# A six-layer decoder on one core: another planner for the order of work, and the context's keys and values made ahead and kept in DRAM

## The chip, the cores and the metric

One Trainium2 chip, of which one core runs the program. TensorE (PE in the profile) does matrix products, VectorE (DVE), ScalarE (ACT) and GpSimd (POOL) do the rest, and SyncE (SP) issues the DMAs. The metric is device microseconds from start to end of one execution, the median of several runs.

## The reference

`x` holds 128 sequences of 64 tokens of 128 numbers, `ctx` the same for a context. Each of six layers adds to `x` something made of `layernorm(x)`:

```python
x = x + mamba2_block(ln(x))                 # scan over 64 steps, then an MLP with silu
x = x + pointers(ln(x), ctx, ids, ptr)      # three rows of ctx by pointer: scores, softmax, values
x = x + ternary_ffn(ln(x))                  # weights of -1, 0, 1; 8-bit activations; gelu
x = x + causal_attention_twice(ln(x))       # 16 heads; the second pass has its queries from a convolution of the first
x = x + cross_attention(ln(x), ctx, mask)   # 16 heads: q of x, k and v of ctx
x = x + experts(ln(x))                      # 8 experts, the two best weighted
```

In the pointers layer `k = ctx @ Wk.T` and `v = ctx @ Wv.T` for two sets of weights; the kernel folds them with the query and output weights into `wqk` and `wvo`. In cross attention `k = ctx @ wk`, `v = ctx @ wv`. These four products need the context alone, and nothing of `x`.

## The kernel before, in words

The 128 sequences are worked in 16 groups of 8 (512 tokens, four tiles of 128x128 in f32). A group goes through ten stages: prepare, project, recur and mlp (the Mamba layer), pointers, ternary, first, second (the two passes of causal attention), cross, experts. `way(g)` (L1603) loads x, calls the stages in turn and stores the result. Up to seven groups are under way at a time (seven buffers `x`), and a stage holds one group at a time: its name is a token that the next group must get.

Nothing at run time decides the order. While the program is built, a class `Turns` (L85) plays the groups against each other, each as a Python generator. `yield V, 0.8` asks for an engine for a planned time in us; `yield "a"` takes a token (a buffer, one of four PSUM banks `a`, the stage's name), `turns.give("a")` hands it back; `yield None, 2.5` lets planned time pass, for a DMA; `yield [p, q]` starts parts side by side. Whoever is chosen issues its instructions at that moment, so that each engine's queue, and SP's queue of DMAs, is written in the order of this play. Each engine then works its queue strictly in that order, held back by semaphores where data or buffers are not ready. The planned lengths are written in by hand (`dv`, `ac`, `po` and literals such as 0.88 for one 128x512 product). Among those who want an engine the planner takes first those who hold a scarce token (`a`, or `s`, the four banks of scores), then the one whose request was made earliest (`process["n"]`); a token goes to whoever asked first.

What the change touches:

- pointers, `group(g)` (L781): takes `ctxT` and one of the two buffers `u`, loads the group's context into it (L786), turns it into `ctxT` by four transposes (`turning`, L317 and L319), stores that in a DRAM tensor `contexts` (L802), makes `kT` by two 128x512 products (`keys`, copied out by ACT at L812) and `vo` by 32 small ones (`outputs`, L828). Beside this the same stage builds one-hot rows on DVE and does the layer norm of x (L307 and L308 on DVE, L286 and L287 and L325 on POOL, then transposes).
- cross, `group(g)` (L1417): loads the mask (L1421), takes `ctxT` and loads it from `contexts` (L1427), makes `km` by one product and two ACT passes (`spreading`, L1086) and `v` by four products (`values`, L214 and L216); beside it the norm and the queries.
- All matrix products are issued in one helper, so that they have the line L210; they are told apart by their tiles.
- project: `arows` is stored to a DRAM tensor `steps` (L484), read back spread over all partitions into four tiles `pT` (L506), which DVE then scans (L530); L572 multiplies the result by a product of PE's.

The buffers `u` are two, shared by the context's load and by all layer norms; from recur to mlp one is held throughout.

Of the kernel before, what the change touches and what calls it, by code (L numbers as in the profile page):

```python
# [32 lines left out]
P = 128  # L33
# [51 lines left out]
class Turns:  # L85
# [5 lines left out]

    LAG = 0.2

    def __init__(self, tokens, scarce=()):
        self.scarce = scarce
        self.free = {name: [0.0] * n for name, n in tokens.items()}
        self.wanted = {name: [] for name in tokens}
        self.asked, self.until, self.now, self.n = {}, {}, 0.0, 0

    def give(self, name):  # L100

        self.running["scarce"] = max(0, self.running["scarce"] - (name in self.scarce))
        if self.wanted[name]:
            _, process = self.wanted[name].pop(0)
            process["time"] = max(process["time"], self.now)
            process["scarce"] += name in self.scarce
            process["engine"] = None
            self.ready.append(process)
        else:
            self.free[name].append(self.now)  # L110

    def process(self, work, time, parent):
        return dict(work=work, time=time, parent=parent, scarce=0, engine=None, n=0)

    def step(self, process):
        self.running = process
        while True:
            self.now = process["time"]
            item = next(process["work"], None)
            self.n += 1  # L120
# [9 lines left out]
            if isinstance(item, str):  # L130
                if not self.free[item]:
                    self.wanted[item].append((self.n, process))
# [11 lines left out]
            else:  # L144
# [9 lines left out]
                else:  # L154
                    process["engine"], process["n"] = engine, self.n
                self.asked.setdefault(engine, []).append((process["scarce"] < 1, process["n"], process, length))
                return

    def run(self, works):
        self.ready = [self.process(work, 0.0, None) for work in works]  # L160
        while True:
# [3 lines left out]
            for engine, asked in self.asked.items():  # L165
                if asked:
                    at = max(self.until.get(engine, 0.0), min(r[2]["at"] for r in asked))
                    first = min((r for r in asked if r[2]["at"] <= at), key=lambda r: r[:2])
# [6 lines left out]
            process, length = request[2:]  # L175
            self.until[engine] = at + length
            process["time"] = at + length + self.LAG
            self.step(process)
        assert not any(self.wanted.values()), {k: v for k, v in self.wanted.items() if v}


@with_exitstack
def tile_decoder(ctx: ExitStack, tc: tile.TileContext, w: dict, const: bass.AP, out: bass.AP):
    nc = tc.nc
    V, A, G, T = nc.vector, nc.scalar, nc.gpsimd, nc.tensor
# [15 lines left out]
    TOKENS.update({name: int(i < 4) for i, name in enumerate(LAYERS)})  # L201
    counter = [0]
# [32 lines left out]
    nc.sync.dma_start(cst, const)  # L235
# [7 lines left out]
    contexts = dram.tile([NG * P, GT], F32, tag="contexts", name="contexts")  # L243
# [17 lines left out]
    for name, v in rows:  # L261
        r = v.shape[0] // P
        nc.sync.dma_start(vrow[at : at + r, :], v.rearrange("(r p) -> r p", p=P))
# [7 lines left out]
    def broadcast(pool, name, ap, n):  # L271

        t = pool.tile([P, n], F32, tag=f"bc_{name}", name=f"bc_{name}")
        nc.sync.dma_start(t, ap.partition_broadcast(P))
        return t

    def load(name, shape, ap, pool):
        t = pool.tile(shape, F32, tag=name, name=name)
        nc.sync.dma_start(t, ap)
# [80 lines left out]
    def natural(shape, ap):  # L360

        t = wk(shape, "pT", bufs=BUFS["pT"])
        nc.sync.dma_start(t, ap)
# [5 lines left out]
    def mamba(mp):  # L369
# [8 lines left out]
        nc.sync.dma_start(taps, w["L0_attn_conv_w"][0:256, :].rearrange("(b p) k -> p b k", p=P))  # L378
# [5 lines left out]
        for i in range(2):  # L384
            rows, of = slice(32 * i, 32 * i + 16), slice(256 + 16 * i, 272 + 16 * i)
            V.tensor_copy(wbc[:, rows], win[:, 512 + 16 * i : 528 + 16 * i])
            nc.sync.dma_start(tbc[rows, :], w["L0_attn_conv_w"][of, :])
            nc.sync.dma_start(bcb[rows, :], w["L0_attn_conv_b"][of].unsqueeze(1))
# [10 lines left out]
        for h in range(4):  # L399
            nc.sync.dma_start(  # L400
# [4 lines left out]
        steps = dram.tile([NC * 4, P], F32, tag="steps", name="steps")  # L405
# [7 lines left out]
        def prepare(g):  # L413
# [70 lines left out]
            nc.sync.dma_start(steps[g * C * 4 : (g + 1) * C * 4, :], rows)  # L484
# [14 lines left out]
        def project(g):  # L499
# [4 lines left out]
            for c in range(C):  # L504
                at = (g * C + c) * 4
                nc.sync.dma_start(  # L506
# [217 lines left out]
    def pointers(mp):  # L724
# [5 lines left out]
        nc.sync.dma_start(pi, w["itok_BxS_0_4092"].rearrange("(c b) s -> c (b s)", b=2))  # L730
        nats = {}
        for names in (("Wout", "Wkj", "Wqj", "Wvj"), ("Wki", "Wqi", "Wvi")):
            t = wk([P, 4, P], "pT", bufs=BUFS["pT"])
            for i, name in enumerate(names):
                nc.sync.dma_start(t[:, i, :], w[f"L0_xattn_{name}"])
# [45 lines left out]
        def group(g):  # L781

            yield "ctxT"
            yield "u"
            cg = wk([P, C, P], "u", bufs=BUFS["u"])
            nc.sync.dma_start(cg, tokens(cf, g))  # L786
            ctxT = wk([P, GT], "ctxT", bufs=BUFS["ctxT"])
            idg = wk([P, C, S], "idg", I32)
            for b in range(2):
                nc.sync.dma_start(  # L790
                    idg[b * S : (b + 1) * S], ids[b, g * C : (g + 1) * C, :].partition_broadcast(S)
                )
            kT = wk([P, B, 2, S], "kT")
            vo = wk([P, B, P], "vo")
            hot = wk([P, 3, C, S], "hot")
            rid = sm([P, C], "rid")

            def context():
                yield None, 2.5
                yield from turning(ctxT, [cg[:, c, :] for c in range(C)])  # L800
                turns.give("u")
                nc.sync.dma_start(contexts[g * P : (g + 1) * P, :], ctxT)  # L802
                yield [keys(0), keys(1), outputs(0), outputs(1)]
                turns.give("ctxT")

            def keys(i):
                yield "a"
                pk = bank("a")
                yield T, 0.88
                mm(pk, wqk[:, i, :], ctxT)  # L810
                yield A, ac(512)
                A.copy(kT[:, :, i, :], pk.rearrange("p (b s) -> p b s", s=S))  # L812
                turns.give("a")

            def outputs(half):
                yield "a"
                pvo = bank("a")
                yield T, 0.95
                for j in range(4):
                    b = half * 4 + j  # L820
                    for i in range(2):
                        mm(
                            pvo[i * S : (i + 1) * S, j * P : (j + 1) * P],
                            ctxT[:, b * S : (b + 1) * S],
                            wvo[:, i, :],
                        )
# [828 lines left out]
```

## Time and profile before

| | |
|---|---|
| median of 3 runs | 2220.43 us (2209.86 to 2229.43) |
| the profiled execution | 2218.08 us, of which the span from first to last instruction is 2216.3 |
| mean granted TensorE clock | 0.931 |
| PE busy | 1925.3 us, 87% of the span |
| PE loading weights (PEld; it overlaps PE) | 1363.1 us, 62% |
| DVE, ACT, POOL busy | 1489.0, 1158.7, 1020.8 us |
| moved by DMA | 53.61 MB, 24 GB/s over the span |

How to read it: engines work side by side, so that busy times do not add up. Idle time of PE is what separates the span from PE's work. A granted clock below 1 means that products of that stretch ran slower than they can. Shares over the whole span hide that the first quarter, in which groups enter one after the other, differs from the rest.

### The profile page before, as it was taken

Reading aid. Unit: us, or ns where it says so; the run is one execution under the profiler, and the core shown is the slowest. Engines: PE = TensorE matmul, PEld = TensorE weight load, DVE = VectorE, ACT = ScalarE, POOL = GpSimd, SP = SyncE. Lnnn points to the kernel's source line nnn. Section 1 sums busy time; section 2 is a strip of 40 time slices with the busy share of each in tenths; the row PEclk is TensorE's granted clock in tenths of the full one; section 3 lists DMA queues with packets and bytes.
Section 4 is the critical chain, followed back from the end, with each engine's and each line's share of the span. In section 5 each row is a group of like instructions: output and inputs, shape, how many; then the busy total and the mean of one; then the engine's idle time right before and its main releaser. Section 6 shows DMA issues by size and latency. Waiting matters only on the chain.

```text
span 2216.3 us, 56830 instructions
## 1 busy us (share of the span) xinstructions
PE 1925.3 (87%) x23920; PEld 1363.1 (62%) x23920; DVE 1489.0 (67%) x3991; ACT 1158.7 (52%) x2133; POOL 1020.8 (46%) x1258
## 2 busy tenths in 40 slices
PE   3777788889889989999998898989889999997996
PEld 1455556566656666666666576666556666675664
DVE  4577877675685676786776847777676765745353
ACT  2345456556464566556565464555655555553452
POOL 2566754743444444364545552464544533423121
PEclk9688898999999999999999899999899999998998
DMA  5011010000010010010001000000000000000000
GB/s 164 20 51 36 28 38 2 23 7 18 22 36 12 6 47 21 16 37 15 26 23 38 6 28 21 16 19 26 28 25 24 2 25 11 17 7 6 12 6 5
DMA packets 73451, 53.61 MB, mean 24 GB/s; under 512 B 30087, under 2 KB 59757, under 8 KB 73197
## 3 DMA queue, kind: packets, MB, share of 16 engines
q1 hardware_dynamic: 73196, 49.99, 7.6%
q8 instruction: 188, 3.08, 0.6%
q14 instruction: 67, 0.54, 0.1%
HBM read 41.45 MB, written 8.52 MB: 23 GB/s over the span
## 4 chain that ended last, share of the span: by engine, by line
PE 55%; DVE 26%; POOL 6%; ACT 6%; issue 3%; DMA 3%; SPq 1%; DVEq 0%; POOLq 0%; ACTq 0%
PE psa L210 38%; PE pss L210 12%; PE psa L317 4%; DVE tops L1212 4%; POOL u L325 2%; DVE amx L1167 2%; DVE pT L1155 2%; DVE x L1581 2%; DVE st L307 1%; ACT pT L1245 1%; DVE mv L308 1%; DVE sel L863 1%; DMA x<-in_x 1%; DVE s L870 1%; DVE mx L1030 1%
## 5 line engine op out<-in xcount | busy, mean ns | idle before, releaser
L325 POOL TENSOR_SCALAR u<-x,mv,rstd 128x128 f32<-128x128 f32 x320 | 252.8, 802 | 52.3 <-PE psa L317 26.0
L210 PE MATMUL psa<-fT,moe_w 128*128 128x512 f32 x512 | 257.8, 627 | 11.3 <-ACT km L559 3.1
L210 PEld LDWEIGHTS psa<-moe_w,hid 128*128 128x128 f32 x2048 | 242.5, 193 | 28.6 <-issue 19.1
L210 PE MATMUL psa<-moe_w,hid 128*128 128x128 f32 x2048 | 252.0, 279 | 2.4 <-DVE sel L863 1.7
L1559 ACT ACTIVATE hid<-psa,vcol 128x512 f32<-128x512 f32 x256 | 173.5, 689 | 147.2 <-PE psa L210 144.4
L1581 DVE SCALAR_TENSOR_TENSOR x<-psa,cw,x 128x128 f32<-128x128 f32 x512 | 143.3, 342 | 127.6 <-PE psa L210 127.5
L1169 POOL TENSOR_TENSOR pT<-pT,amx 128x512 f32<-128x512 f32 x128 | 134.6, 1055 | 185.9 <-DVE amx L1167 177.9
L286 POOL TENSOR_SCALAR rsq<-mv 128x4 f32<-128x4 f32 x96 | 24.7, 257 | 368.6 <-DVE mv L308 346.1
L1245 ACT ACTIVATE pT<-pss 128x512 f32<-128x512 f32 x256 | 132.1, 603 | 118.8 <-PE pss L210 118.7
L1212 DVE TENSOR_REDUCE tops<-pss 128x32 f32<-128x2048 f32 x64 | 146.1, 2283 | 41.3 <-PE pss L210 41.3
L1044 POOL TENSOR_SCALAR r<-h 128x512 bf16<-128x512 f32 x64 | 98.0, 1540 | 128.2 <-DVE h L1042 127.0
L210 PEld LDWEIGHTS psa<-fT,moe_w 128*128 128x128 f32 x512 | 91.3, 198 | 100.2 <-issue 59.4
L1289 DVE TENSOR_TENSOR fT<-psa,inv 128x256 f32<-128x256 f32 x96 | 40.2, 420 | 155.2 <-ACT inv L1287 154.2
L210 PEld LDWEIGHTS pss<-km,qm 32*128 32x128 f32 x3072 | 101.4, 198 | 46.7 <-issue 31.5
L210 PE MATMUL psa<-pT,cst 128*32 128x256 f32 x1536 | 119.6, 401 | 10.4 <-ACT pT L1245 2.9
L625 POOL TENSOR_TENSOR qm<-qm,km 128x256 f32<-128x256 f32 x64 | 51.6, 809 | 165.6 <-DVE qm L620 165.5
L317 PE MATMUL psa<-cst,u 128*128 128x128 f32 x448 | 83.9, 304 | 50.1 <-POOL u L325 33.9
L210 PE MATMUL pss<-km,qm 32*128 32x128 f32 x3072 | 120.6, 297 | 5.6 <-DVE pT L1155 3.5
L307 DVE BATCH_NORM_STATS2 st<-x 128x6 f32<-128x128 f32 x384 | 102.7, 267 | 20.6 <-DMA x<-in_x 20.1
L319 ACT COPY fT<-psa 128x512 f32<-128x512 f32 x112 | 65.7, 588 | 85.2 <-PE psa L317 84.8
L317 PEld LDWEIGHTS psa<-cst,u 128*128 128x128 f32 x448 | 56.0, 151 | 78.2 <-POOL u L325 43.3
L1285 ACT ACTIVATE inv<-psa 128x256 f32<-128x256 f32 x96 | 37.0, 385 | 125.9 <-PE psa L210 125.5
(282 smaller groups left out, 4621.3 us busy)
## 6 DMA issues: line engine op xcount, KB each, us to landing
pT<-steps SPq DMA_DIRECT2D x64, 256.0 KB, 4.0
x<-in_x SPq DMA_DIRECT2D x16, 256.0 KB, 2.8
mask<-in_mask_Bx1xSxS_ff SPq DMA_DIRECT2D x32, 128.0 KB, 3.0
u<-in_ctx SPq DMA_DIRECT2D x16, 256.0 KB, 2.7
contexts<-ctxT SPq DMA_DIRECT2D x16, 256.0 KB, 2.0
ctxT<-contexts SPq DMA_DIRECT2D x16, 256.0 KB
out<-x SPq DMA_DIRECT2D x16, 256.0 KB, 2.3
idg<-in_itok_BxS SPq DMA_DIRECT2D x32, 64.0 KB, 2.8
```

Of the source, the lines that this page charges most:

```text
L210: T.matmul(o, lhsT=lhsT, rhs=rhs, start=start, stop=stop)
L307: V.bn_stats(st[:, c, :], X[:, c, :])
L317: T.transpose(pt[:, c * P : (c + 1) * P], part, by)
L319: A.copy(o, pt)
L325: G.tensor_scalar(u[:, c, :], X[:, c, :], mean(c), scale[:, c : c + 1], ALU.subtract, ALU.mult)
L625: G.tensor_tensor(xc[:, :, cols], xc[:, :, cols], zs[:, :, cols], ALU.mult)
L1044: G.tensor_scalar(r2, h[:, c, :], -MAGIC, None, ALU.add)
L1169: G.tensor_tensor(s3, s3, mx.unsqueeze(2).to_broadcast([P, 8, S]), ALU.subtract)
L1212: V.tensor_reduce(mx[:, :, 0:8], banks.rearrange("p r (n s) -> p r n s", s=S), AX.X, ALU.max)
L1245: A.activation(pTs[r].rearrange("p b g q -> p (b g q)"), banks[:, r, :], AF.Exp)
L1559: A.activation(hid[:, b, :], ph, AF.Relu, bias=vec["moe_b1"][:, 2 * e + b : 2 * e + b + 1])
L1581: V.scalar_tensor_tensor(X[:, c, :], po_[:, c * P : (c + 1) * P], cw[:, c, e : e + 1], X[:, c, :], ALU.mult, ALU.add,)
```

## The change

1. **Context ahead.** The stage pointers makes no keys any more. A new process `ahead()` goes through the 16 contexts on its own: load into a buffer of the tag `ctxT`, transposes, then `kT` and `vo` (for pointers) and `km` and `v_x` (for cross), each stored in a DRAM tensor of its own per group (4 KB a partition for `kT`, `vo` and `km`, 6 KB for `v_x`). The stages pointers and cross load these back. `contexts` is gone, and the context no longer takes a buffer `u`. One buffer each of `kT`, `vo` and `v_x` serves both sides, by tokens; `km` shares its four. A token `pointed{g}` or `crossed{g}` lets the stage of group g begin only when its tensors were made. `ahead` has rank 1, all groups have rank 0: it gets an engine or a token only where no group wants it, except while it holds a bank.
2. **Planning with TensorE's clock.** The planner cuts time into stretches of 3.413 us; a product of PE's is planned at half speed unless PE was planned busy for 0.74 of the stretch before.
3. **Allowances.** Requests are ordered by rank, then by the time at which they are made plus an allowance of the layer. `planned` plays the whole program 150 times with allowances altered at random and keeps what ends earliest; in these plays the engines issue nothing (`Engine`, `Stand`). In the program built from it the allowances are: cross -19.2, recur -14.3, ternary -14.3, project -12.5, experts -5.6, mlp -5.2, first -0.8, second 0, pointers +6.2, prepare +6.7.

The number of products, and of all other instructions on PE, is the same in both. The diff, cut to its core (`nc.sync` is renamed to `Q` throughout):

```diff
     LAG = 0.2
+    STRETCH, ENOUGH = 3.413, 0.74
+    def taken(self, engine, at, length):
+        if engine is not self.clocked:
+            return length
+        t, left = at, length
+        while left > 1e-9:
+            i = int(t / self.STRETCH + 1e-9)
+            rate = 1.0 if self.worked.get(i - 1, 0.0) >= self.ENOUGH * self.STRETCH else 0.5
+            part = min((i + 1) * self.STRETCH - t, left / rate)
+            self.worked[i] = self.worked.get(i, 0.0) + part
+            left -= part * rate
+            t += part
+        return t - at
+    def layer(self, name):
+        self.running["allowance"] = self.allowances.get(name, 0.0)
...
-            _, process = self.wanted[name].pop(0)
+            first = min(self.wanted[name], key=lambda w: w[0])
...
+    def age(self, process):
+        self.n += 1
+        return process["rank"], process["time"] + process["allowance"], self.n
...
-            self.until[engine] = at + length
+            self.until[engine] = at + self.taken(engine, at, length)
...
+def planned(layers, names, rounds=150):
+    chance = random.Random(2)
+    best, end = {}, layers({})
+    for _ in range(rounds):
+        tried = dict(best)
+        for name in chance.sample(names, chance.choice((1, 2, 3))):
+            tried[name] = round(tried.get(name, 0.0) + chance.uniform(-15.0, 15.0), 1)
+        at = layers(tried)
+        if at <= end:
+            best, end = tried, at
+    return best
...
+    TOKENS.update(ctxT=1, kT=1, vo=1, v_x=1, laid=0)
+    TOKENS.update({f"{name}{g}": 0 for name in ("pointed", "crossed") for g in range(NG)})
...
@@ pointers: group(g) @@
-            yield "ctxT"
-            yield "u"
-            cg = wk([P, C, P], "u", bufs=BUFS["u"])
-            nc.sync.dma_start(cg, tokens(cf, g))
-            ctxT = wk([P, GT], "ctxT", bufs=BUFS["ctxT"])
+            yield f"pointed{g}"
+            yield "kT"
+            kT = wk([P, B, 2, S], "kT", bufs=1)
+            Q.dma_start(kT.rearrange("p b i s -> p (b i s)"), kept["kT", g])
+            yield "vo"
+            vo = wk([P, B, P], "vo", bufs=1)
+            Q.dma_start(vo.rearrange("p b d -> p (b d)"), kept["vo", g])
...
-            yield [context(), ones(), norming_T(xs[g], uT)]
+            yield [ones(), norming_T(xs[g], uT)]
...
@@ cross: of_context(g, ctxT), new @@
+        def of_context(g, ctxT):
+            def keys():
+                yield "km"
+                km = wk([P, B, 2, S], "km", bufs=BUFS["km"])
+                yield from spreading(km, wkk, ctxT, k["mk"], None)
+                Q.dma_start(kept["km", g], km.rearrange("p b i s -> p (b i s)"))
+                yield None, 3.0
+                turns.give("km")
+            def of_values():
+                yield "v_x"
+                yield from values(vs[0], ctxT, wv)
+                Q.dma_start(kept["v_x", g], vs[0])
+                yield None, 4.0
+                turns.give("v_x")
+            yield [keys(), of_values()]
+            turns.give(f"crossed{g}")
...
@@ cross: group(g) @@
-            yield "ctxT"
-            ctxT = wk([P, GT], "ctxT", bufs=BUFS["ctxT"])
-            nc.sync.dma_start(ctxT, contexts[g * P : (g + 1) * P, :])
+            yield f"crossed{g}"
+            yield "v_x"
             v = vs[0]
+            Q.dma_start(v, kept["v_x", g])
             yield "km"
             km = wk([P, B, 2, S], "km", bufs=BUFS["km"])
+            Q.dma_start(km.rearrange("p b i s -> p (b i s)"), kept["km", g])
...
+    def ahead():
+        def loaded(g):
+            cg = wk([P, C, P], "ctxT", bufs=2)
+            Q.dma_start(cg, tokens(cf, g))
+            return cg
+        yield "laid"
+        following = loaded(0)
+        yield None, 2.5
+        for g in range(NG):
+            cg = following
+            ctxT = wk([P, GT], "ctxT", bufs=2)
+            yield from turning(ctxT, [cg[:, c, :] for c in range(C)])
+            if g + 1 < NG:
+                following = loaded(g + 1)
+            yield [stages["pointers ahead"](g, ctxT), stages["cross ahead"](g, ctxT)]
...
-    turns.__init__(TOKENS, ("a", "s"))
+        turns.__init__(TOKENS, ("a", "s"), T, allowances)
...
-        turns.run([way(g) for g in range(NG)] + [weights()])
+        return turns.run([(0, way(g)) for g in range(NG)] + [(0, weights()), (1, ahead())])
```

## The prediction

> **What bounds the kernel now.** I read the page first, for busy shares and slices.
>
> ```profile
> span 2216.3 us, 56830 instructions
> PE 1925.3 (87%) x23920; PEld 1363.1 (62%) x23920; DVE 1489.0 (67%) x3991; ACT 1158.7 (52%) x2133; POOL 1020.8 (46%) x1258
> ...
> PE   3777788889889989999998898989889999997996
> DVE  4577877675685676786776847777676765745353
> ...
> PEclk9688898999999999999999899999899999998998
> ```
>
> PE is the bound, but not in the first eight slices, where it is busy seven or eight tenths at a lower clock. So the second view is a table of stretches: columns are us, busy time of PE, PEld, DVE, ACT, POOL, then the granted clock.
>
> ```profile
> 55.40:110.80 55.40, 39.01 (x147) 24.43 (x148) 30.40 (x92) 17.70 (x37) 31.48 (x39) 0.62 0.06 20
> 110.80:166.20 55.40, 40.99 (x243) 28.09 (x244) 44.03 (x114) 25.39 (x46) 33.59 (x45) 0.82 0.15 51
> 166.20:221.60 55.40, 41.98 (x245) 27.78 (x243) 43.67 (x109) 33.11 (x54) 38.61 (x50) 0.85 0.12 36
> ...
> 1551.40:1773.00 221.60, 198.33 (x2543) 141.98 (x2542) 157.56 (x422) 124.67 (x227) 109.43 (x135) 0.95 0.06 19
> 1773.00:1994.70 221.70, 207.69 (x3118) 150.01 (x3111) 134.40 (x341) 122.99 (x224) 77.41 (x86) 0.96 0.05 15
> ```
>
> The timeline of SP gives the cut between the two regimes: seven groups are let in at once, and the eighth gets its buffer x when the first is stored, at 560 us. Cut there, the table is:
>
> ```profile
> 0.00:560.00 560.00, 430.34 (x4524) 295.80 (x4525) 392.02 (x1046) 279.02 (x513) 303.39 (x383) 0.88 0.13 38
> 560.00:2216.30 1656.30, 1494.94 (x19398) 1067.30 (x19396) 1096.97 (x2946) 879.70 (x1621) 717.43 (x875) 0.95 0.07 19
> ```
>
> Before 560 us PE is idle for 129.7 us of 560 (23%), after it for 161.4 of 1656.3 (9.7%): the fill waits on the latency of single groups, the rest on PE. SP's timeline also shows a context at work: loaded into a buffer u (L786), stored when it has left it (L802).
>
> ```profile
> 560.20 0.39 SPq L1613 DMA_DIRECT2D out<-x  x1
> ...
> 580.40 0.37 SPq L786 DMA_DIRECT2D u<-in_ctx  x1
> 604.50 0.33 SPq L484 DMA_DIRECT2D steps<-arows  x1
> 606.96 1.76 SPq L506 DMA_DIRECT2D pT<-steps  x4
> ...
> 623.71 0.43 SPq L802 DMA_DIRECT2D contexts<-ctxT  x1
> ```
>
> Last, the groups by form that the context costs on PE (busy us, mean ns), and two DMAs (us to landing):
>
> ```profile
> L210 PE MATMUL psa<-wvo,ctxT 128*64 128x128 f32 x512 | 34.7, 288 | 2.3 <-DVE fT L1289 1.2 <-ACT kT L812 1.1
> L210 PE MATMUL psa<-ctxT,wqk 128*128 128x512 f32 x64 | 34.0, 646 | 2.4 <-ACT ctxT L319 2.0 <-ACT r2T L319 0.3
> L317 PE MATMUL psa<-cst,u 128*128 128x128 f32 x448 | 83.9, 304 | 50.1 <-POOL u L325 33.9 <-DVE u L678 10.0 <-DMA u<-in_ctx 2.6
> L210 PE MATMUL psa<-ctxT,x_wk 128*128 128x512 f32 x32 | 17.5, 627 | 0.0
> L210 PE MATMUL psa<-x_wv,ctxT 128*128 128x128 f32 x128 | 17.0, 275 | 0.0
> ```
>
> ```profile
> pT<-steps SPq DMA_DIRECT2D x64, 256.0 KB, 4.0
> ...
> contexts<-ctxT SPq DMA_DIRECT2D x16, 256.0 KB, 2.0
> ```
>
> **Part 1, context moved into the fill.** A group's context costs PE 34.0 + 34.7 + 17.5 + 17.0 us over 16 groups and 64 of the 448 transposes (83.9 / 7 = 12.0): 115.2 / 16 = 7.2 us, nothing of it new. What counts is where it stands. In PE's old order, ahead of group 7's first product (the 560 us mark), are the transposes, wqk and wvo of six contexts (80.7 / 16 x 6 = 30.3 us) and the cross part of two (34.5 / 16 x 2 = 4.3): 34.6. In the new order nine whole contexts are: 64.8. So 30.2 us of PE work leave the stretch in which PE is busy 90.3%: 30.2 / 0.903 = -33 us. In the fill they cost between 0 (all in PE's idle 129.7 us) and 30.2 / (430.34 / 560) = +39 (nothing hidden). I take +10: PE, ACT (32 to 60% busy in the three stretches) and POOL have room, DVE (79% in two of them) gets only the copies it had anyway.
>
> **Clock in the fill.** From 55 to 222 us PE is busy 122.0 us at a mean clock of 0.76; where it is busy over 83% it was granted 0.92 and more. With more work between, the clock can stay (0) or come to 0.95 (122 x 0.76 / 0.95: -24). I take -6, a quarter, since chains that wait on DVE win nothing. The Trainium skill (TensorE: Matmul & The Clock Gate, Part 1) has the clock at half unless a window of about 3.4 us was busy; by it, filling nearly every window would give the whole 24 and a sum 18 us lower. The trace agrees in that busier stretches have the higher clock (0.62 at 70% busy, 0.96 at 94%); that the gaps close, nothing here shows.
>
> **Part 2, order of the rest: clock in the plan, allowances, no u.** Allowances of -19 (cross) to +7 (prepare) make almost a ranking of the stages, as a request seldom waits that long. No row shows the new order, so I bound it by stretches. After 560 us 1494.9 - 30.2 = 1464.7 us of PE work are left: at 90.3% 1622 us, at the best stretch's share (207.69 / 221.7 = 93.7%) 1563, at the worst's (89.5%) 1637. So -59 to +15, middle -22. One thing speaks for the gaining side: from L786 to L802 a context held one of the two buffers u for 5 to 44 us (580 to 624 above), 262 us over 16, and PE's transposes wait 33.9 us for POOL to write u. I take -30.
>
> **DMA.** 128 transfers come (64 stores, 64 loads; 512 KB, for v_x 768) and 32 of 256 KB go. SP issues one in 0.4 us: 38 us more of SP's 2216, which is mostly waiting. By size from 4.0 us for 256 KB a load lands within 8, v_x within 12. They are covered: kT by the norm in the same stage (4 x (267 + 182) ns on DVE, 257 + 1049 and 4 x 802 on POOL, 4 x 304 transposes, 588 copy: 8.1 us); km by that and the queries; v by the scores and the softmax too. ACT's copies, DVE's and POOL's work are moved, not added. I take 0; without the cover each group's chain is some 4 us longer, 64 in all, part of the last rival.
>
> **Sum** against the profiled 2218.1 (2.3 below the median 2220.4): 2218.1 - 33 + 10 - 6 - 30 = 2159, say **2160**. The good ends together: 2218.1 - 33 + 0 - 24 - 59 = 2102; the bad ends: 2218.1 - 33 + 39 + 0 + 15 = 2239.
>
> **Rivals.**
> *Larger gain*: good ends, 2102. For it: idle and half clock are there to be had. Against it: the plan's lengths are still guesses (0.88 for a 128x512 product, while wqk's 32 took 34.0 us, 1.06 each).
> *Nothing at the end*: the fill pays for its contexts in full and the order is only different: 2218 - 33 + 39 = 2224. For it: PE is already busy 77% before 560 us, DVE 79% in places. Against: PE's 31 idle us from 55 to 166, and that the nine contexts do stand early in PE's new order, so that the change does what it says.
> *SP's queue, slower*: the new order has on SP, for groups 7 to 15, `v_x` stored and at once, into the same tile, another group's `v_x` loaded; SP stands till the store has landed, and behind it wait stores to `steps`, loads of `pT`, masks. Price: 12 us of landing by size, and some 4 for data that the low rank makes late; DVE's first scan came in the middle 8 us after its load was issued, 4 of them landing, so 4 are slack. Nine groups x 12 us = 108: 2160 + 108 = 2268. It decides once SP is held over 4 + 58 / 9 = 10 us a group. Against it: now SP stands up to 69 us at one wait, and the scans waited 1.9 us for DMA in all. The Trainium skill (DMA: Bandwidth & Descriptors, Two DMAs through the same engine are not ordered) says the issuing engine must wait out such a store, which is this mechanism; its fit in Anatomy of one DMA (2.0 us + bytes / 436,000, for GpSimd's path) estimates 3.8 us for v_x instead of my 12, by which the rival would be nearly gone. No row here has a transfer of 768 KB.
>
> **Chances.** A measurement tells about 1% from no change. Forecast (2120 to 2195) 0.52; larger gain 0.13; nothing 0.17; slower 0.18, the SP queue being most of it. So faster by over 1% 0.65, same 0.17, slower 0.18. For 8 in 10 I reach from just below the good ends, 2095, to just above the bad ones, 2245.
>
> **What would show it.** Right: the first `out` still near 560 us, with PE over 450 us busy before it and a clock of 0.9 from 55 to 222; after it a PE share of 92% or more; no L530 waiting for `pT<-steps`. Part 1 is wrong if the first `out` comes 30 us or more later; part 2 if the share after it stays at 90%; the DMA's zero if DVE or PE wait for `steps`, `kT` or `v_x`.

## The result, and the profile after

The changed kernel takes 2200.5 us (median of 8 runs, 2193.3 to 2202.3), the kernel before 2217.8 beside it: ratio 0.9919, 95% interval 0.9899 to 0.9939. That is 17 us where about 60 were forecast, and within the 1% that the prediction counts as no change. The page of the changed kernel:

```profile
span 2198.8 us, 57057 instructions
...
PE 1906.6 (87%) x23915; PEld 1352.6 (62%) x23920; DVE 1474.3 (67%) x3991; ACT 1163.1 (53%) x2134; POOL 1005.9 (46%) x1258
...
PE   3787678899998898989998989789988889898996
...
PEclk9888789999999999999999999889999999999998
```

PE's share has stayed at 87%, and slices of 7 and 8 still stand in the second half, in other places than before. The stretches of the prediction (us, busy time of PE, PEld, DVE, ACT, POOL, granted clock):

```profile
55.40:110.80 55.40, 43.20 (x245) 28.29 (x244) 36.94 (x95) 31.94 (x61) 29.66 (x44) 0.82 0.44 158
110.80:166.20 55.40, 45.50 (x238) 28.26 (x237) 41.78 (x119) 28.31 (x56) 31.68 (x40) 0.86 0.42 149
166.20:221.60 55.40, 43.36 (x259) 30.50 (x257) 40.68 (x114) 27.94 (x50) 30.60 (x45) 0.84 0.16 60
0.00:560.00 560.00, 436.72 (x4533) 298.31 (x4538) 380.31 (x1023) 294.71 (x542) 294.88 (x387) 0.90 0.27 89
560.00:2198.80 1638.80, 1469.90 (x19387) 1054.32 (x19387) 1093.98 (x2968) 868.37 (x1593) 711.02 (x871) 0.95 0.13 43
```

The fill did what was expected of it: between 55 and 222 us PE is busy 132.1 us instead of 122.0, at a higher clock. The rest did not: its share of PE is 89.7%, where it was 90.3%. The first group is stored before the 560 us mark. It is the out in this timeline of SP (start, length, line, transfer):

```profile
536.32 0.56 SPq L864 DMA_DIRECT2D kT<-kT  x1
538.62 0.39 SPq L1729 DMA_DIRECT2D out<-x  x1
539.06 0.60 SPq L1542 DMA_DIRECT2D mask<-in_mask_Bx1xSxS_ff  x1
541.94 0.38 SPq L1721 DMA_DIRECT2D x<-in_x  x1
```

539 instead of 560, and the second group at 658 instead of 691. This lead does not last: the third group is stored at 843 instead of 803, the ninth at 1577 instead of 1557, and the last two at 2141 and 2195 instead of 2159 and 2213.

**Where PE's time goes.** The clock of each moment is in the trace, full or half. So the span can be cut into three parts that add up: PE's work as it would be at full clock (busy time less half of the busy time at half clock), what half clock adds, and PE's idle time. Taking half is fair: in the changed kernel's trace 128x512 products that follow each other directly start every 429 ns (median) in full-clock moments and every 854 ns in half-clock ones. Before: 1802.1 + 123.2 + 291.0 = 2216.3. After: 1796.2 + 110.4 + 292.2 = 2198.8. The work is the same to 6 us, 12.8 us come from half clock, nothing from idle time. Cut at 560 us: the fill did 393.9 us of full-clock work instead of 378.0, and after it 21.6 us less work was left, but its idle time rose from 161.3 to 168.9.

### The profile page after: what moved, and what is told of

The parts are those of the page before. It is cut to its first block, busy times and chain, and to the rows that moved or that the text cites. A ratio compares the mean times of both kernels' runs of the same rounds, so it can differ in the third digit from the quotient of the medians.

```text
span 2198.8 us, 57057 instructions
## 1 busy us (share of the span) xinstructions
PE 1906.6 (87%) x23915; PEld 1352.6 (62%) x23920; DVE 1474.3 (67%) x3991; ACT 1163.1 (53%) x2134; POOL 1005.9 (46%) x1258
## 2 busy tenths in 40 slices
DMA packets 87277, 120.75 MB, mean 55 GB/s; under 512 B 31622, under 2 KB 61292, under 8 KB 87020
## 4 chain that ended last, share of the span: by engine, by line
PE 52%; DVE 25%; POOL 9%; ACT 7%; DMA 3%; issue 3%; SPq 1%; DVEq 0%; POOLq 0%; ACTq 0%
PE psa L285 37%; PE pss L285 11%; PE psa L396 4%; POOL u L404 3%; DVE tops L1310 3%; DVE pT L1253 1%; DVE amx L1265 1%; DVE pT L609 1%; DVE st L386 1%; DMA x<-in_x 1%; DVE x L1700 1%; DVE sel L909 1%; DVE mv L387 1%; DVE s L916 1%; POOL r L1142 1%
## 5 line engine op out<-in xcount | busy, mean ns | idle before, releaser
L365 POOL TENSOR_SCALAR rsq<-mv 128x4 f32<-128x4 f32 x96 | 21.6, 225 | 538.9 <-DVE mv L387 532.2
L1343 ACT ACTIVATE pT<-pss 128x512 f32<-128x512 f32 x256 | 137.3, 604 | 104.4 <-PE pss L285 104.2
L285 PE MATMUL psa<-pT,cst 128*32 128x256 f32 x1536 | 113.0, 404 | 3.8 <-DVE u L735 1.5
L1269 ACT ACTIVATE pT<-pT 128x512 f32<-128x512 f32 x128 | 79.8, 632 | 68.5 <-POOL pT L1267 68.0
L396 PE MATMUL psa<-cst,u 128*128 128x128 f32 x384 | 72.9, 299 | 30.6 <-POOL u L404 22.9
L1253 DVE TENSOR_TENSOR pT<-pss,mask 128x512 f32<-128x512 f32 x128 | 87.3, 682 | 15.3 <-PE pss L285 15.2
```

The costliest lines, as they stand in the source:

```text
L285: T.matmul(o, lhsT=lhsT, rhs=rhs, start=start, stop=stop)
L396: T.transpose(pt[:, c * P : (c + 1) * P], part, by)
L1253: V.tensor_tensor(sco, banks[:, r].rearrange("p (b h s) -> p b h s", b=4, s=S), mask[:, 4 * quad : 4 * quad + 4, :].unsqueeze(2).to_broadc ...
L1269: A.activation(sco, sco, AF.Exp)
L1343: A.activation(pTs[r].rearrange("p b g q -> p (b g q)"), banks[:, r, :], AF.Exp)
```

## The experiments

The reasons tried, with the letters that some expectations use: (A) moving PE's work of the context into the fill is the gain; (B) the chip follows the end that the planner works out for its own plan, whatever the change is; (C) the order's end is an accident, some 20 us either way, for reasons that the plan does not show; (D) a context made late would have served as filler; (E) a context that is made ahead at rank 1 holds a single buffer (kT, vo, v_x) while its requests lose to everything at rank 0, and the stages wait for the buffer. All results at one place; "plan" is the end that the kernel's own planner gives its order (a number of the program, not of the chip), us is the median, idle and half clock are the two parts of the span above, of one profiled execution each:

| run | context | clock in plan | plannings | plan | us | ratio to before | idle | half clock |
|---|---|---|---|---|---|---|---|---|
| before | in stage | no | none | 2117 | 2217.8 | 1 | 291 | 123 |
| changed kernel | ahead | yes | 150 | 2137 | 2200.5 | 0.9919 [0.9899, 0.9939] | 292 | 110 |
| e1 | ahead | no | none | 2122 | 2274.4 | 1.0263 [1.0238, 1.0288] | 330 | 140 |
| e2 | ahead | yes | none | 2240 | 2263.0 | 1.0212 [1.0192, 1.0233] | 332 | 123 |
| e3 | in stage | yes | 150 | 2147 | 2208.0 | 0.9964 [0.9944, 0.9985] | 298 | 106 |
| e4 | ahead | no | 150 | 2045 | 2186.2 | 0.9856 [0.9832, 0.9881] | 276 | 114 |
| e5 | 15 of 16 left out | yes | after's | 2148 | 2178.4 | 0.9840 [0.9823, 0.9857] | 314 | 151 |
| e6 | ahead, later | no | none | 2123 | 2267.3 | 1.0251 [1.0216, 1.0286] | 315 | 138 |
| e7 | ahead, rank raised | no | none | 2100 | 2225.5 | 1.0043 [1.0024, 1.0061] | 297 | 126 |
| e8 | in stage | no | none | 2109 | 2214.0 | 1.0003 [0.9987, 1.0020] | 288 | 129 |
| e9 | ahead, rank raised | no | 600 | 1996 | 2150.5 | 0.9689 [0.9666, 0.9711] | 249 | 118 |
| e10 | ahead, rank raised | yes | after's | 2137 | 2184.0 | 0.9827 [0.9804, 0.9849] | 269 | 110 |
| e11 | in stage | no | 150 | 2058 | 2170.4 | 0.9772 [0.9750, 0.9794] | 267 | 100 |
| e12 | ahead | no | 150, seed 3 | 2058 | 2212.9 | 0.9955 [0.9939, 0.9972] | 286 | 136 |
| f1 | ahead | yes | 150, seed 3 | 2152 | 2232.8 | 1.0061 [1.0042, 1.0080] | 300 | 141 |
| f2 | ahead | yes | 150, seed 4 | 2144 | 2244.1 | 1.0107 [1.0085, 1.0130] | 314 | 129 |
| f3 | in stage | no | 600 | 2041 | 2166.6 | 0.9750 [0.9721, 0.9779] | 259 | 119 |
| f4 | ahead, rank raised | no | 150 | 2022 | 2183.2 | 0.9850 [0.9822, 0.9877] | 277 | 122 |
| g1 | ahead, rank raised | yes | f1's | 2226 | 2245.5 | 1.0138 [1.0122, 1.0154] | 317 | 122 |
| g2 | ahead, rank raised | yes | f2's | 2202 | 2285.2 | 1.0323 [1.0306, 1.0340] | 333 | 151 |

PE's work at full clock is 1785 to 1811 us in every row but e5 (1711). Everything else is idle time and half clock.

### The parts by themselves (e1 to e4)

```diff
-        turns.__init__(TOKENS, ("a", "s"), T, allowances)
+        turns.__init__(TOKENS, ("a", "s"), None, allowances)     # e1 and e4: no clock
...
-    best = planned(layers, LAYERS)
+    best = {}                                                    # e1 and e2: no search
```

e3 keeps clock and search and puts each context back into its stages, with the stores and loads of the kernel before.

> Context ahead as in the changed kernel, but the planner plans TensorE at full speed and with no allowances. Theory A (the context's place is the gain, orders otherwise matter little): 2185 to 2200 us, like the changed kernel, and the first output near 540 us. Theory B (the chip follows the plan, whose end this part leaves where it was: 2122 planned, 2117 for the kernel before): 2215 to 2235. A third, that the context ahead harms by itself and the search mends it: over 2240.

> The changed kernel without the search: context ahead and TensorE's clock in the plan, all allowances zero. Its plan ends at 2240, that of the changed kernel at 2137, which became a span of 2199 on the chip (1.029 times the plan). Theory A: the allowances move little, 2195 to 2215. Theory B: the chip follows the plan, 2240 x 1.029 = 2305, so between 2280 and 2320, and the search then is worth about 100 us, which planning with the clock had first to lose.

> The other half alone: the context made inside the stages pointers and cross as before, with the clock in the plan and its own search of 150 plays (other allowances come of it; its plan ends at 2147). Theory A: no gain without the context moved, 2210 to 2230. Theory B: 2147 x 1.029 = 2209, so 2200 to 2215, and the context ahead is worth the remaining 10 us.

> Context ahead and a search of 150 plays, but planned with TensorE at full speed; the plan ends at 2045. The kernel before, planned in that way too, took 1.047 times its plan. Theory B (any plan that ends earlier ends earlier on the chip): 2045 x 1.047 = 2141, so 2125 to 2160. Theory A: 2185 to 2205. Against both, a third theory, that a search tuned to a TensorE which is always fast finds what the real one does not keep: 2215 or more.

Contexts ahead and nothing else makes the kernel 57 us slower (e1), and the search more than makes up for it (e4: 88 us less than e1). So moving the work brought no gain by itself in this order, and (A) falls as the reason for the 17 us. e1 stores its first group at 522 us, earlier than the changed kernel, and still ends last of the four. Of the forecasts, e1 bears out the third alone (over 2240). e2 lies between (A) and (B), e3 in the range of (B) and 2 us below that of (A). e4 lies in the range of (A), far above that of (B); that a search without the clock would do harm is wrong.

The page of e1 shows the loss in PE's share, spread over the second half (7 and 8 in most slices from 23 to 35):

```profile
span 2268.8 us, 57066 instructions
...
PE 1938.4 (85%) x23919; PEld 1367.8 (60%) x23920; DVE 1478.9 (65%) x3991; ACT 1159.4 (51%) x2134; POOL 1023.7 (45%) x1258
...
PE   3787778798899998988999798898799888799996
```

### Is PE's work the bound, and is it the planner? (e5, e8)

e5 is the changed kernel with its own allowances, but it computes the context of group 0 alone, and every group loads that one: 15 of 16 contexts are left out, with 15 x 7.2 = 108 us of PE's work by the prediction's own price. e8 has the new planner without clock and search, and the contexts in their stages.

```diff
         for g in range(NG):
+            if g:
+                turns.give(f"pointed{g}")
+                turns.give(f"crossed{g}")
+                continue
...
-            Q.dma_start(kT.rearrange("p b i s -> p (b i s)"), kept["kT", g])
+            Q.dma_start(kT.rearrange("p b i s -> p (b i s)"), kept["kT", 0])
```

> The changed kernel with its own allowances, but the keys and values of the first group's context alone are made, and all groups load those (15 of 16 contexts are left out of the computation). 15 x 7.2 = 108 us of TensorE's work are gone, the order is planned anew. Theory A (TensorE's work is the bound, and moved work counts by its length): 2200 - 108 / 0.9 = 2080, so 2060 to 2110. Theory C (what decides is how well the stages' chains happen to fit into each other; the contexts fill gaps that stay open without them, and allowances fit one set of work only): the plan ends at 2148, later than with all contexts (2137), so 2190 to 2225.

> The kernel before in the new planner: context in its stages, TensorE at full speed, no allowances. All that is left of the change is that requests are ordered by the time at which they are made instead of by the count of the planner's steps. The plan ends at 2109 instead of 2117. Theories A, D and E: no change, 2205 to 2225. Theory C (orders of equal worth to the planner scatter by tens of us on the chip): more than 20 us off, to either side.

```profile
span 2175.9 us, 55216 instructions
...
PE 1862.3 (86%) x23167; PEld 1320.5 (61%) x23170; DVE 1457.2 (67%) x3961; ACT 1094.1 (50%) x1999; POOL 1020.8 (47%) x1258
...
PE   3576788889888989989998989979898989898896
...
PEclk9677799999988989899998999999999999998998
```

This page of e5 is the one that tells most. 85.0 us of full-clock work are gone (1796.2 to 1711.2; the 108 are more, since in the changed kernel 20 of the 119 us of context products overlap with other products and 17 ran at half clock), and the kernel is only 22 us faster than the changed one (18 by the ratios): PE's share falls to 86%, idle time grows by 21 us, half clock by 41. In this order a microsecond of PE work taken away brought 22 / 85 = 0.26 us of time, though PE is 87% busy. That is one order, planned anew with allowances found for other work, so 0.26 is no price to be used elsewhere; but (A), which asked for 2060 to 2110, is out by 68 us. (C) asked for 2190 to 2225 and is out by 12. PE is busiest, but most of what it was spared came back as gaps and half clock. e8 agrees with the kernel before to 0.03%: in this order the new planner costs nothing. (A), (D) and (E) had forecast that; (C), which asked for a change of more than 20 us, missed.

### Is it the low rank? (e6, e7, e10, g1, g2)

In e1 the time from a context's first product with wqk to the store of kT, some 3 us in the first groups, is 49 and 65 us in two late ones; over 16 groups 188 us for kT, and likewise 87 for vo, 128 for v_x. For kT a stage's load follows the store within 3 us in eight of the 16 groups, which suggests that it had been waiting. e6 lets context g start only once group g has its x; e7 raises the process's rank as soon as it holds a buffer.

```diff
                 yield "kT"
+                turns.running["rank"] = 0        # the same for vo and v_x: e7, e10, g1, g2
```

> e1 (context ahead, TensorE planned at full speed, no allowances; 2274) with one more rule: the context of a group is made only once that group has its buffer x, so that contexts 7 to 15 come some 200 us later and still fill gaps at the end. Theory D (e1 is slow since contexts made early are missing as filler later): 2215 to 2245, with the gain after 1000 us. Theory C (an accident of the order; the plan ends at 2123, as e1's 2122): anywhere from 2220 to 2290, with no such pattern.

> e1 with the process that makes the contexts raised to the rank of the groups as soon as it holds one of the shared single buffers kT, vo or v_x. Theory E (e1 is slow since stages wait for a buffer held by work that comes last everywhere): 2215 to 2240; the plan ends at 2100 instead of 2122. Theory C: it moves by the plan's 22 us at the most, 2245 to 2270, or anywhere.

e7 took the holding down to 60, 56 and 95 us and 49 of the 57 us with it, which looked like (E), in whose range it lies; e6 moved little, against (D). So the same edit was made in the changed kernel (e10), and, when other seeds had been run, in two more orders of it (g1, g2), in which the allowances no longer fit and the plan ends later.

> The changed kernel with its clock and its own allowances, and only the rank of the holders of kT, vo and v_x raised to 0. The plan ends at 2137.3, the changed kernel's own at 2137.2. If the end of the plan decides: 2200, as the changed kernel. If holding the buffers at a low rank costs on the chip what the plan does not show (first product to store of kT 176 us over 16 groups): 2165 to 2190. If the allowances fit only the order they were found for: 2210 or more.

> The changed kernel with the allowances of seed 3 (2232.8 us) and the holders of kT, vo and v_x raised to rank 0. The plan ends at 2226 us instead of 2152. If the chip follows the plan: 2232.8 x 2226 / 2152 = 2310. If the inversion cost time on the chip whatever the plan says: 16 to 49 less than 2232.8, so 2184 to 2217. If a change of order at this level is chance: within 20 of 2232.8.

> The changed kernel with the allowances of seed 4 (2244.1 us) and the holders of kT, vo and v_x raised to rank 0. The plan ends at 2202 us instead of 2144. By the plan 2244.1 x 2202 / 2144 = 2305. By the inversion 2195 to 2228. By chance within 20 of 2244.1.

e10 gained 16 us, but g1 lost 13 and g2 41 us (differences of the medians), although the holding fell there as well (kT from 126 to 61 us in g1, from 151 to 71 in g2). e10 lies in the range of (E), g1 in that of chance, g2 in none of its three. So (E) is not shown as the general cause: -49, -16, +13 and +41 us for one edit may be no more than what another order brings. Nor is it excluded: in those four the plan's end moved by -22, 0, +74 and +58, and g1 and g2 lost less than their later plans asked for (2310 and 2305 us), so that a gain from shorter holding may be hidden in them.

### Context ahead or in its stages, and how much of it is the seed (e9, e11, e12, f1 to f4)

```diff
-    chance = random.Random(2)
+    chance = random.Random(3)       # e12 (no clock) and f1; 4 in f2
...
-def planned(layers, names, rounds=150):
+def planned(layers, names, rounds=600):     # e9 and f3
```

e11 is e3 without the clock in the plan, f3 the same with 600 plannings; e9 and f4 are e7 with a search of 600 and of 150. e11 and e12 run their search; e9 and f1 to f4 carry the allowances that theirs found, written in as `best`.

> Context ahead, holders of kT, vo and v_x raised to rank 0 as in the run without the inversion, no clock in the plan, and the allowances of a search of 600 plannings (the plan ends at 1996 us; the search of 150 with the inversion, 2186 us on the chip, ends at 2045). Theory that the chip follows the plan: orders planned without the clock took 1.05 to 1.07 of their plan, so 2096 to 2136. Theory of the held buffers alone (the search had mended most of the holding by itself): 2170 to 2186. Rival, that more search only fits the plan's wrong lengths: 2186 or more.

> The context in its stages as before, search of 150 plannings without the clock (plan 2058 us; context ahead with the same search 2045 planned, 2186 measured). If making the context ahead is worth what the plan says: 2186 x 2058 / 2045 = 2200. If the place of the context is worth nothing and no holding of single buffers can occur: 2170 to 2186. If it is worth the 33 less 10 us of the prediction: 2209 or more.

> Context ahead, search of 150 plannings without the clock, with another seed of the search's random numbers (plan 2058 us instead of 2045; allowances wholly different). It sizes the accident in a found order: by the plan 2186 x 2058 / 2045 = 2200. If the measured end has a scatter of its own of about 15 us, somewhere from 2180 to 2220; within 8 us of 2200 means that the plan's end tells orders of one kind apart to that much.

> The changed kernel, nothing else changed than the seed of its search (plan 2152 us, the changed kernel's 2137). By the plan 2200 x 2152 / 2137 = 2215. If the 18 us belong to the change: 2190 to 2210. If they are the luck of one order: a scatter as between the two seeds without the clock, so anywhere from 2180 to 2235.

> The changed kernel with a third seed of its search (plan 2144 us). By the plan 2207. If the 18 us belong to the change: 2190 to 2210. If they are the luck of one order: from 2180 to 2235, and the mean of the three seeds tells what the change is worth.

> The context in its stages, a search of 600 plannings without the clock (plan 2041 us; the search of 150 had 2058 and took 2170). By the plan 2170 x 2041 / 2058 = 2152. If making the context ahead is worth something once nothing holds its buffers: 2160 or more, 10 or more above the 2150.5 of the same search ahead. If its place is worth nothing: 2140 to 2160.

> Context ahead without the inversion, search of 150 plannings without the clock (plan 2022 us; its search of 600 had 1996 and took 2150.5). By the plan 2150.5 x 2022 / 1996 = 2178. If the inversion was what kept the context ahead from paying: 2155 to 2165, below the 2170 of the same search in the stages. If the longer search only had luck: 2175 or more.

The changed kernel with two other seeds of the same search takes 2233 and 2244 us, more than the kernel before; the intervals of the three ratios lie apart. Their mean is (0.9919 + 1.0061 + 1.0107) / 3 = 1.003. So the 17 us belong to the order that one seed hit upon, which is (C): two of three orders of the same change have none of it. Three seeds are few, with ratios 0.019 apart, so a small mean gain or loss of the change stays possible.

Of the forecasts, e11 lies in the range for a place that is worth nothing, e12 and f1 in the range for scatter, f2 9 us above it. e9 lies in none, between the plan's and that of the held buffers. f3 and f4 point opposite ways: f3, 16 us above e9, in the range for contexts ahead that are worth something once nothing holds their buffers, and f4, 13 us above e11, in the one for mere luck of the longer search.

What the fill holds does not decide either. Here are stretches of f2 (contexts ahead, 2244 us):

```profile
0.00:560.00 560.00, 434.36 (x4334) 299.72 (x4334) 385.98 (x1044) 298.48 (x544) 302.11 (x379) 0.91 0.29 96
560.00:2244.20 1684.20, 1495.73 (x19587) 1066.20 (x19587) 1097.88 (x2947) 864.23 (x1591) 724.13 (x879) 0.94 0.12 40
```

and of e11 (contexts in their stages, 2170 us):

```profile
0.00:560.00 560.00, 415.79 (x4382) 280.82 (x4385) 392.90 (x1039) 276.29 (x505) 307.50 (x391) 0.87 0.13 38
560.00:2165.50 1605.50, 1482.62 (x19536) 1059.62 (x19536) 1084.61 (x2952) 887.25 (x1630) 707.22 (x867) 0.96 0.07 20
```

At 560 us f2 is ahead by 393.2 - 363.2 = 30.0 us of full-clock work, as much as the prediction had moved, and has a clock of 0.91 against 0.87. It ends 79 us later: after the mark it has 28 us less of full-clock work to do, but PE is idle for 188.5 us there and for 122.9 in e11 (88.8% and 92.3% busy), and half clock adds 88 us there and 47 in e11.

Three comparisons over several orders say more than any one run, though they share orders, and most of the differences are below the 44 us (2%) between three seeds:

- Search. Against its own structure without one, a search was faster in all seven cases of 150 plannings that have such a partner (changed kernel, f1, f2 against e2; e4, e12 against e1; e11 against e8; f4 against e7), by 1 to 4%: 1.0% (f2) to 4.0% (e4).
- Clock in the plan. With the search, the plan with the clock gave the slower kernel in all three pairs: e4 to the changed kernel +0.6%, e12 to f1 +1.1%, e11 to e3 +2.0%. It did not spare half clock: 110, 141 and 106 us with it, 114, 136 and 100 without. Without a search e2 is 0.5% below e1, with 123 us of half clock instead of 140. Three pairs do not show that the clock in the plan is to blame.
- Ahead against in its stages, same planner. Without a search +2.6%, with the rank raised +0.4%; 150 plannings without the clock +0.9 and +1.9%, with the rank raised +0.8%; with the clock -0.5, +1.0 and +1.4%; 600 plannings, rank raised (ahead only), -0.6%. Seven of nine are slower, but the contexts in their stages have only one order for each way of planning, and no second seed. (e10, g1 and g2, whose allowances were found without the raised rank, are at -1.4, +1.8 and +3.6% of e3.)

The plan's end is a rough guide: over the ten runs from e1 on without the clock in the plan its correlation with the span is 0.86, and a line through them leaves a scatter of 22 us; over the eight with it (the changed kernel among them, e5 not) 0.72 and 26 us. So orders whose plans differ by 20 us can't be told apart by the plan, and (B) holds for large differences alone. e9, the order with the earliest plan, is also the fastest: 2150.5 us, 3.1% below the kernel before and 2.3% below the changed one. Its page, of an execution that took 2160.2 us:

```profile
span 2158.2 us, 56959 instructions
...
PE 1909.2 (88%) x23915; PEld 1347.6 (62%) x23920; DVE 1487.8 (69%) x3991; ACT 1158.9 (54%) x2134; POOL 1025.2 (48%) x1258
...
PE   3787689899999899989989898998989899999996
```

It is the same work with 249 us of idle PE time, where the changed kernel has 292.

## Why the prediction was right or wrong

**Part 1, -33: the step that failed.** The moving was right and its price wrong. Nine contexts do stand before the 560 us mark in the new order, and after it PE is busy 25.0 us less (1494.9 to 1469.9), where 30.2 were forecast. But "30.2 / 0.903 = -33 us" took PE for the bound after the mark: it lets the time shrink with PE's work at an unchanged busy share, and that share did not hold. e1 has Part 1 alone, for which the sum has -33 + 10 - 6 = -29 us. It took 57 us more, and after 560 us PE was busy 88.4% (1510.7 of 1708.8 us), not 90.3%. e5 shows the same without any moving: of 85 us of PE work taken away, 62 came back as idle time and half clock. The nine comparisons, from -0.6 to +2.6%, show no steady gain from the place of the contexts. The step rested on a reading: 90.3% busy was taken for "the rest on PE", when the 9.7% idle and the half clock depend on the order and change with it.

**The cost in the fill, +10.** Too high here: the first group left 22 us earlier, not later, and PE had been busy 419.6 us by then, not the 450 of the prediction's mark. The third group was already 40 us later than before, so the first `out` says little about the end.

**Clock in the fill, -6.** Right in kind and size. Half clock cost 30.7 us between 55 and 222 us before and 22.3 after: -8.4. The Trainium skill (TensorE: Matmul & The Clock Gate, Part 1) has the clock at half unless a window of about 3.4 us was busy, and with nearly every window filled the prediction had up to 24 us for it; the trace agrees with the direction (0.62 to 0.82 where PE rose from 39.0 to 43.2 us), but the windows were not all filled: PE was still idle for 34.1 of the 166.2 us, where it had been 44.2. It did not decide the end: e11 has 0.68, 0.78 and 0.75 in those stretches and is 30 us faster.

**Part 2, -30: mis-sized, by the same step.** Here too busy time was turned into time by a share of PE's that was taken as known. The share after 560 us was to rise to 92% or more, and it fell to 89.7%. That is still within the bounds (89.5 to 93.7%), at the bad end: by the prediction's own rule it costs 10 us (1469.9 us of work take 1638.8 us; at the 90.26% of before they would take 1628.5) where -30 were forecast. In the terms of the sum this is most of the miss in the changed kernel: -25.0 / 0.9026 = -27.7 us for the work that left and +10.3 for the share give the 17.5 us (rounded) by which the stretch after 560 us became shorter. It was not to be read from the profile, as three seeds of the same rule lie 44 us apart: the whole change came to -17, +12 and +24 us (medians, against the kernel before beside each). The "middle" of two bounds was a single number where only a spread was known. The "one thing" that "speaks for the gaining side", the buffer u, was small: PE's transposes wait for POOL's u 22.9 us instead of 33.9, and they are 64 fewer.

```profile
L396 PE MATMUL psa<-cst,u 128*128 128x128 f32 x384 | 72.9, 299 | 30.6 <-POOL u L404 22.9 <-ACT hid L1678 2.2 <-ACT v_a L289 1.9
```

**DMA, 0.** Right for the changed kernel, although the bytes moved rose from 53.61 to 120.75 MB: no engine's wait for a load of kT, vo, km or v_x stands in the trace, and the one new wait for a context is 12.5 us of PE's for the first. The landing times (tile and tensor, transfers, KB each, median us from issue to landing; half of the 32 are stores):

```profile
v_x<-v_x SPq DMA_DIRECT2D x32, 768.0 KB, 4.1
kT<-kT SPq DMA_DIRECT2D x32, 512.0 KB, 3.0
vo<-vo SPq DMA_DIRECT2D x32, 512.0 KB, 4.3
pT<-steps SPq DMA_DIRECT2D x64, 256.0 KB, 3.8
```

These medians rest on few transfers, as the trace tells the landing of only some: five loads of v_x (4.0 to 4.4 us) and three stores (3.2 to 3.3), and one load each of kT (3.4), vo (4.3) and km (5.9). So 768 KB landed there in 4.4 us at most, not the 12 by size (in f2 one store of v_x took 7.2). The Trainium skill's fit (DMA: Bandwidth & Descriptors, Anatomy of one DMA) gave an estimate of 3.8 us for v_x, and the trace comes near it. The one load of km took longer, 5.9 us, though it is smaller (512 KB), so that size alone does not tell the time.

**The rivals.** SP's queue: false. SP stood at the load of v_x (L1549) behind its store nine times, 3.9 us at most, not 12. For data that the low rank makes late it stood longer than the rival had it, at its stores of kT (L997) and v_x (L1531) up to 43.8 and 25.0 us. But what lay behind was hardly missed: the scans (L530 before, L609 now) wait 4.4 us in all for the steps, where they had waited 1.9. The lines (SP's: us in all, times, longest):

```profile
SPq L1531 <- DVE v_x L291: 148.9, 14, 25.0
SPq L997 <- ACT kT L1011: 110.0, 11, 43.8
SPq L1549 <- DMA v_x<-v_x: 27.4, 9, 3.9
...
L609 DVE TENSOR_TENSOR_SCAN pT<-pT,eye 128x512 f32<-128x512 f32 x64 | 79.6, 1282 | 4.4 <-DMA pT<-steps 4.4
```

Larger gain: idle time and half clock were to be had, as it said, but by better orders (e9, e11), not by this change, and not down to 2102. Nothing at the end, 2224: that its number is the mean of the three seeds (1.003 x 2217.8 = 2224) is luck. Half of its reason ("the order is only different") is what happened; the other half, that the fill pays in full, did not. A rival that was missing came nearest: that the end of an order scatters by some 25 us about what its plan says, whatever is moved.

**Still open.** Which waits make one order 70 us longer than another with the same work was not found: holding single buffers was tried, and the four runs with the raised rank do not settle it. Whether the plan with the clock finds worse orders, and why, is open as well, and so is the price of PE's work beyond the one order of e5. A different seed was tried for e4 and for the changed kernel only, so the spread of the others is assumed to be alike.

## What to carry to other kernels

An engine that is 87% busy is not yet the bound: take work away from it in one run before you price moved work at its share, since here, in the one order measured, 85 us less of it brought 22. Where a planner or a search lays down the order, one measurement of a changed rule is one draw; run the same rule under two or three seeds before you give the difference to the rule, and compare it with the structure before under the same search. A search over such orders can be worth more than the change that it comes with (e11 keeps the contexts where they were and takes 2170 us).

## What the runs showed of the hardware that was not expected

The landing time did not go by size in the few transfers whose landing the changed kernel's trace tells: 2.7 us for 256 KB of context, 3.3 to 5.1 for 256 KB of pT, 3.4, 4.3 and 5.9 for loads of 512 KB, 4.0 to 4.4 for loads of 768. And the half clock is not a matter of the fill alone: over whole spans it added 100 to 151 us of some 2200, and of the changed kernel's 110.4 us, 67.5 fall after 560 us, where PE is 90% busy and the granted clock reads 0.95. No long pause is needed for it: in the traces of the kernel before, the changed one, e1, e11 and f2 the clock fell to half 222 times, and the longest idle stretch of PE in the 6.8 us before was 1.9 us in the median case, with PE busy for 41% of the last 3.4 us. So gaps that an order leaves can cost twice, once as idle time and once as half clock behind them (in e5 21 and 41 us more).
